# Cross-attention's key mask: from PE matmuls into the keys' last row

## The chip, the cores and the metric

The kernel runs on one core of a Trainium2 chip. The core has a matrix engine (PE, TensorE), a vector engine (DVE), a scalar engine (ACT), a general one (POOL, GpSimd) and a queue that only issues DMAs here (SP). The metric is device time in microseconds. The kernel before took 2411.13 us, the median of three runs (2407.03 to 2411.5).

## The reference, cut to what matters

Four attention blocks follow one another on a batch of 8 sequences of 256 rows and 128 features. The third, L2, holds nearly all of the time: six layers, each with self-attention, cross-attention to 64 context rows of 64 features, and a feed-forward part. The change touches cross-attention alone:

```python
tn = _ln(t, norm_g, norm_b)
t = _mha(src, tn, ckv, cq, cow, cob, src_mask) + t
# _ln(x, g, b):  (x - m) / jnp.sqrt(v + eps) * g + b
# in _mha, 16 heads of 64:
q = t @ q_w
k, v = jnp.split(s @ kv_w, 2, axis=-1)
scores = jnp.einsum('bhqd,bhkd->bhqk', q, k) * D ** (-0.5)
scores = jnp.where(mask[:, None] == 0, jnp.float32(-1000000000.0), scores)
attn = jax.nn.softmax(scores, axis=-1)
```

The mask has one row of 64 keys for each sequence, the same for all heads and queries.

## The kernel before, in words

**Folded weights.** Each layer multiplies the query weights into the key weights (`AT`) and the output weights into the value weights (`WVO`) once, in `plan_ca_weights`. A sequence's keys are then `AT` times its context: a tile of 128 features by 16 heads by 64 keys, made in `keys_both` for two sequences at a time. Scores are the normalised rows, turned so that features lie on the partitions (`tT`), times these keys.

**Ticks and phases.** The program is a list of steps. `at(tick, phase, step)` files a step; at the end all steps are recorded in order of tick, then of phase, and that order is forced on PE, DVE, ACT and POOL each. Every one of these engines so runs strictly in the order of the plan, whatever is ready; only SP's DMAs are placed by the scheduler. Self-attention takes four ticks for a sequence, cross-attention two. Below, T is the first tick of a layer's cross-attention (`T_ca` in the code), so sequence b has the ticks T+2b and T+2b+1, and self-attention of the last sequence starts at T-4.

**One cross-attention tick** (`plan_weights_64`, with a mask): PE makes scores (phase 1); ACT copies them out of PSUM (L372), DVE takes the maximum for each head (L374), POOL subtracts it (L375) (phase 2); ACT takes the exponential (L381, phase 8). In the next tick DVE sums and inverts (L385, L386) and POOL multiplies (L387) (phase 2.4). In the tick after that DVE transposes (L395, phase 2.5), and in the third PE multiplies by the values (`sums`, L429, phase 3). A scores step is 16 matmuls of 128 rows by 32 columns with 256 moving columns in float32 (L356), four at a time on the four column groups of the array, and behind each four of them four more in bfloat16 (L363) that add the mask: a row of ones times a row with 0 or -1e30. Each float32 matmul has two records in the trace.

**Normalisation** (`ahead`): DVE takes the moments, POOL the inverse root (L859, L862), ACT normalises (L868), PE transposes (L882), and ACT takes the transpose out of PSUM with the norm's scale and bias (L884). Self-attention of the next layer does its normalising on DVE (L873), at phase 2.6, behind that tick's transposes.

**One self-attention tick**: DVE adds the mask and takes the maximum in eight instructions (L953), ACT takes exponentials (L958), DVE inverts their sums (L966), POOL divides (L968), DVE transposes (L978), PE multiplies by the values (L994). `out_proj` is L1012, its addition L1019.

**PSUM** is a ring of four buffers of two banks: each new tile takes the buffer of the fourth tile before it, and waits until that one was read. The heap's tags ("q", "o", "k", "e") are rings of four in SBUF in the same way.

**The weights of a layer's cross-attention**, with W = T-6 as the start: DVE transposes them (L1057) at W-6 and W-5; SP sends them through DRAM and back (L1060, L1068); POOL regroups them (L1074) at W+1, phase 8.05; PE makes `AT` at W+2 and `WVO` at W+3, both at phase 3.6 (L1083), and ACT takes them out of PSUM (L1095, L1093). The first `keys_both` (L1120, copied out by L1126) is at T-2, phase 3.7.

Of the kernel before, what the change touches and what calls it, by code (L numbers as in the profile page):

```python
# [8 lines left out]
F32 = mybir.dt.float32  # L9
I32 = mybir.dt.int32  # L10
BF16 = mybir.dt.bfloat16
# [5 lines left out]
P = 128  # L17
# [10 lines left out]
def tile_xattn_stack(ctx: ExitStack, tc: tile.TileContext, io, out: bass.AP):  # L28
# [124 lines left out]

    norm_g = column("L2_norm_g")
    norm_b = column("L2_norm_b")
    pre_g = load_const("L2_pre_gT", [D, NL])
    pre_b = load_const("L2_pre_bT", [D, NL])
    ff_b1 = load_const("L2_ff_b1T", [P, NL, FF // P])
# [103 lines left out]
        return nm  # L262


    nm2 = const.tile([P, B, M], BF16, tag="nm2", name="nm2")
    nc.vector.memset(nm2, 0.0)
    ones0 = const.tile([P, 32], BF16, tag="ones0", name="ones0")
    nc.vector.memset(ones0, 0.0)
    nc.vector.memset(ones0[0:1], 1.0)


    def stats(xin, eps):
# [21 lines left out]
    def at(tick, phase, fn):  # L294
        plan.setdefault(tick, []).append((phase, fn))
# [30 lines left out]
        )  # L326
        return vw

    def plan_weights_64(tick, qt, qT, keys, values, mask, take):

        tl = {}

        def scores():
            sc = two_banks("sc").rearrange("p (q x) -> p q x", q=4)
            if mask is None:
                for i in range(4):
                    for a in range(4):
                        q = (i + 2 * (a // 2)) % 4  # L340
                        rows = slice(64 * (a // 2), 64 * (a // 2) + 64)
                        qb = 4 * qt + q
                        nc.tensor.matmul(
                            sc[32 * a : 32 * a + 32, q, :],
                            lhsT=qT()[rows, qb * 32 : (qb + 1) * 32],
                            rhs=keys()[rows, 4 * (a % 2) : 4 * (a % 2) + 4, :].rearrange(
                                "p h k -> p (h k)"
                            ),
                            start=True, stop=True,
                        )  # L350
                tl["sc"] = sc.rearrange("p q x -> p (q x)")
                return
            for q in range(4):
                qb = 4 * qt + q
                for a in range(4):
                    nc.tensor.matmul(  # L356
                        sc[32 * a : 32 * a + 32, q, :],
                        lhsT=qT()[:, qb * 32 : (qb + 1) * 32],
                        rhs=keys()[:, a].rearrange("p h k -> p (h k)"),
                        start=True, stop=False,  # L360
                    )
                for a in range(4):
                    nc.tensor.matmul(  # L363
                        sc[32 * a : 32 * a + 32, q, :], lhsT=ones0, rhs=mask,
                        start=False, stop=True,
                    )
            tl["sc"] = sc.rearrange("p q x -> p (q x)")

        def lower():
            sc = tl.pop("sc")  # L370
            e = big("e", shape=(P, 16, M))
            nc.scalar.copy(e.rearrange("p h k -> p (h k)"), sc)  # L372
            m = sm([P, 16], "m16")
            nc.vector.tensor_reduce(m, e, AX.X, ALU.max)  # L374
            nc.gpsimd.tensor_tensor(  # L375
                e, e, m.unsqueeze(2).to_broadcast([P, 16, M]), ALU.subtract
            )
            tl["e"] = e

        def exps():  # L380
            nc.scalar.activation(tl["e"], tl["e"], AF.Exp)  # L381

        def divide():
            r = sm([P, 16], "r16")
            nc.vector.tensor_reduce(r, tl["e"], AX.X, ALU.add)  # L385
            nc.vector.reciprocal(r, r)  # L386
            nc.gpsimd.tensor_tensor(  # L387
                tl["e"], tl["e"], r.unsqueeze(2).to_broadcast([P, 16, M]), ALU.mult
            )

        def turn():
            e = tl.pop("e").rearrange("p (q h) (k x) -> p (h k) q x", q=4, x=32)
            eT = big("k" if mask is None else "o", shape=(P, 8, 4, 32))
            for i in range(2):
                nc.vector.transpose(eT[:, 4 * i : 4 * i + 4], e[:, 4 * i : 4 * i + 4])  # L395
            tl["eT"] = eT

        def sums_by_head():

            ps = two_banks("mm").rearrange("p (i x) -> p i x", i=2)  # L400
            eT, vw = tl.pop("eT"), values()
            for i in range(2):
                for k in range(2):
                    for j in range(4):
                        nc.tensor.matmul(
                            ps[32 * j : 32 * j + 32, i, :P],
                            lhsT=cones.rearrange("p a f -> p (a f)") if i == 0
                            else vw[:, 4 * k + j, :],
                            rhs=eT[:, 2 * j + k].rearrange("p q x -> p (q x)"),
                            start=(k == 0), stop=(k == 1),  # L410
                        )
# [24 lines left out]
        at(tick, 2, lower)  # L436
        if mask is None:
            at(tick + 1, 2.05, exps)
            at(tick + 1, 2.5, turn)
            at(tick + 2, 1.9, sums_by_head)  # L440
            at(tick + 2, 4.6, outputs)
        else:
            at(tick, 8, exps)
            at(tick + 1, 2.4, divide)
            at(tick + 2, 2.5, turn)
            at(tick + 3, 3.0, sums)
# [188 lines left out]

    def mask_keys():
        mi = big("q", dtype=I32)
        mi = mi[0:1, : B * M].rearrange("p (b m) -> p b m", b=B)
        nc.sync.dma_start(out=mi, in_=io["mask_Bx1xS2_if1"].rearrange("b o m -> o b m"))
        nc.vector.tensor_scalar(nm2[0:1], mi, 0.0, -BIG, ALU.is_equal, ALU.mult)  # L640

    mask_bf = []

# [39 lines left out]
    def plan_l0(b, T):  # L683
# [87 lines left out]
        at(T + 1, 3.2, make_values)  # L771
        for qt in range(QT):
            plan_weights_64(
                T + qt, qt, lambda: st["q"], lambda: st["k"], lambda: st["VW"], None,
                lambda ps, qt=qt: add(qt, ps),
            )
        at(T + 3, 6, moments)
# [268 lines left out]
    def plan_ca_weights(l, T):  # L1046
# [54 lines left out]
            at(T - 4 + i, -0.5, lambda i=i: fetched(i))  # L1101
        at(T + 1, 8.05, regrouped)
        at(T + 2, 3.6, folded("AT", 0, lambda c: st[1][:, :, c, :], HD ** -0.5))
        at(T + 3, 3.6, folded("WVO", 1, lambda c: W["ca", l][2][:, c, :]))

    keys_of = {}

    def plan_ca(l, b, T):
# [3 lines left out]
        def keys_both():  # L1112
# [16 lines left out]
                    )  # L1129
            keys_of[b], keys_of[b + 1] = res  # L1130

        def make_values():
            st["VW"] = values_of(b, fold["WVO"])

        def res():
            st["tb"] = residual(b, W["ca", l][3])

        ahead(b, (T - 4, 6), (T - 3, 2.95), (T - 2, 2.9), norm_g, norm_b, st)
        if b % 2 == 0:
            at(T - 2, 3.7, keys_both)  # L1140
        at(T + 2, 3.2, make_values)
        at(T + 2, 7, res)

        def add(qt, ps):
            nc.vector.tensor_add(t[:, QT * b + qt, :], ps[:, :D], st["tb"][:, qt, :])  # L1145

        for qt in range(QT):
            plan_weights_64(
                T + qt, qt, lambda: st["tT"], lambda: keys_of[b], lambda: st["VW"],
                nm2[:, b].unsqueeze(1).to_broadcast([P, 4, M]), lambda ps, qt=qt: add(qt, ps),  # L1150
            )

    def plan_ff(l, b, T, T_second, steps=None):
# [117 lines left out]
    for l in range(NL):  # L1271
        T_ca = T0 + 4 * B
        T_next = T_ca + 2 * B
        for b in range(B):
            plan_sa(l, b, T0 + 4 * b)
        plan_ca_weights(l, T_ca - 6)
        for b in range(B):
            plan_ca(l, b, T_ca + 2 * b)
            T_ff = T_ca + 2 * b + 7
# [101 lines left out]
```

## Time and profile before

| what | value |
|---|---|
| median of three runs | 2411.13 us |
| the profiled execution | 2410.29 us, span 2408.5 us, mean PE clock 0.987 |
| ACT busy | 1707.7 us, 71% |
| POOL busy | 1359.1 us, 56% |
| weight loads of PE (PEld) | 1719.9 us, 71% |

The profile is of one execution. Its rows give for a group of equal instructions the busy time and the mean duration of one in ns, and behind the last bar how long the engine had been idle before them and what ended that. Matmuls overlap, so that a mean duration is not what one costs; the distance between starts is.

The second layer is followed as the example. In its timeline the scores of the ticks start at these times, in us:

| tick | T-5 | T-4 | T-3 | T-2 | T-1 | T | T+1 | T+2 | T+3 | T+4 |
|---|---|---|---|---|---|---|---|---|---|---|
| start | 731.33 | 738.72 | 743.33 | 752.00 | 760.31 | 765.84 | 768.50 | 775.41 | 785.28 | 789.56 |

| tick | T+5 | T+6 | T+7 | T+8 | T+9 | T+10 | T+11 | T+12 | T+13 | T+14 | T+15 |
|---|---|---|---|---|---|---|---|---|---|---|---|
| start | 795.06 | 799.35 | 810.68 | 816.70 | 822.47 | 830.27 | 837.95 | 847.54 | 858.62 | 868.15 | 875.38 |

### The profile page before, as it was taken

How to read it: one execution, taken by the hardware profiler on the slowest of the kernel's cores; microseconds unless marked ns; L12 is line 12 of the kernel's file. 1: busy time of each engine (PE TensorE's matmuls, PEld its weight loads, DVE VectorE, ACT ScalarE, POOL GpSimd, SP SyncE). 2: the span in 40 equal slices, each digit the busy share in tenths (PEclk: the TensorE clock that was granted, in tenths of full speed). 3: DMA queues.
4: the chain of work that ended last, by engine and by line, in shares of the span. 5: the costliest groups of instructions: out<-in, count | busy, mean ns of one | idle time of the engine just before them, and what ended most of it. 6: DMA issues, size and time to landing. Idle time of an engine off the chain costs nothing.

```text
span 2408.5 us, 100346 instructions
## 1 busy us (share of the span) xinstructions
PE 2325.2 (97%) x42564; PEld 1719.9 (71%) x42564; DVE 1872.3 (78%) x6237; ACT 1707.7 (71%) x4514; POOL 1359.1 (56%) x2231
## 2 busy tenths in 40 slices
PE   7889999999999999999999999999999999999997
PEld 4557777777777777777777777777777777777775
DVE  5677887777888767888767888767888767888775
ACT  4567777667777667778667778667778667777663
POOL 2444556754556754555764555755555765455665
PEclk9989999999999999999999999999999999999998
DMA  6000022001022001012000012000013000001000
GB/s 180 2 2 20 21 73 65 2 3 30 21 64 66 11 3 30 21 56 73 12 2 26 21 45 87 12 2 18 25 40 89 21 2 18 25 26 42 2 4 16
DMA packets 102834, 76.90 MB, mean 32 GB/s; under 512 B 8113, under 2 KB 96881, under 8 KB 102386
## 3 DMA queue, kind: packets, MB, share of 16 engines
q1 hardware_dynamic: 101794, 70.16, 10.1%
q8 instruction: 335, 5.49, 0.9%
q14 instruction: 113, 0.93, 0.1%
q10 hardware_dynamic: 592, 0.33, 0.1%
HBM read 62.07 MB, written 8.39 MB: 29 GB/s over the span
## 4 chain that ended last, share of the span: by engine, by line
PE 75%; DVE 13%; ACT 5%; POOL 4%; issue 2%; DMA 0%; SPq 0%; POOLq 0%; ACTq 0%; DVEq 0%
PE sc L939 12%; PE mm L902 12%; PE mm L994 12%; PE mm L1012 6%; PE mm L921 6%; PE mm L429 6%; PE sc L356 5%; DVE e L953 3%; PE mm L1178 3%; PE mm L1161 3%; DVE eTc L978 2%; DVE m L374 2%; POOL e L968 2%; PE mm L1120 2%; PE mm L318 2%
## 5 line engine op out<-in xcount | busy, mean ns | idle before, releaser
L968 POOL TENSOR_SCALAR e<-e,rs 128x256 f32<-128x256 f32 x1536 | 702.8, 478 | 706.3 <-DVE rs L966 696.5
L958 ACT ACTIVATE e<-e,mn 128x256 f32<-128x256 f32 x1536 | 758.6, 495 | 151.3 <-DVE mn L953 146.5
L953 DVE CUSTOM_DVE_ANT_0 e<-sc,nm 128x256 f32<-128x256 f32 x1536 | 543.1, 419 | 93.4 <-PE sc L939 92.3
L978 DVE STREAM_TRANSPOSE eTc<-e 128x512 f32<-128x512 f32 x768 | 516.2, 694 | 59.4 <-POOL e L968 58.2
L939 PE MATMUL sc<-k,q 64*32 64x256 f32 x12288 | 380.8, 383 | 2.3 <-DVE o L299 1.3
L994 PE MATMUL mm<-eTc,v 32*64 32x256 f32 x12288 | 363.4, 378 | 5.7 <-ACT AT L1095 3.3
L375 POOL TENSOR_TENSOR e<-e,m 128x1024 f32<-128x1024 f32 x112 | 213.0, 1902 | 262.1 <-DVE m L374 262.1
L994 PEld LDWEIGHTS mm<-eTc,v 32*64 32x64 f32 x12288 | 277.1, 131 | 88.5 <-issue 22.2
L939 PEld LDWEIGHTS sc<-k,q 64*32 64x32 f32 x12288 | 221.8, 107 | 125.3 <-issue 51.4
L374 DVE TENSOR_REDUCE m<-e 128x16 f32<-128x1024 f32 x112 | 136.3, 1217 | 197.0 <-ACT e L372 197.0
L958 ACT ACTIVATION_READ_ACCUMULATOR e<-e,mn 128x1 f32 x1536 | 287.9, 187 | 0.0
L356 PE MATMUL sc<-q,tT 128*32 128x256 f32 x3072 | 217.0, 382 | 3.8 <-DVE t L1019 3.2
L429 PE MATMUL mm<-v,o 128*128 128x128 f32 x1536 | 197.5, 283 | 1.9 <-DVE t L1145 1.7
L429 PEld LDWEIGHTS mm<-v,o 128*128 128x128 f32 x1536 | 183.1, 195 | 19.0 <-issue 9.1
L902 PE MATMUL mm<-tT,w_sk 128*128 128x256 f32 x768 | 189.2, 389 | 0.2 <-PE mm L994 0.2
L1012 PEld LDWEIGHTS mm<-w_sow,o 128*128 128x128 f32 x1536 | 175.1, 192 | 17.6 <-issue 12.3
L921 PE MATMUL mm<-w_sv,tT 128*32 128x256 f32 x3072 | 185.6, 382 | 0.0
L1012 PE MATMUL mm<-w_sow,o 128*128 128x128 f32 x1536 | 183.6, 278 | 1.3 <-ACT WVO L1093 1.3
L387 POOL TENSOR_TENSOR e<-e,r 128x1024 f32<-128x1024 f32 x96 | 182.6, 1902 | 0.5 <-DVE r L386 0.5
L301 ACT COPY v<-mm 128x1024 f32<-128x1024 f32 x96 | 97.1, 1012 | 115.4 <-PE mm L921 115.4
L902 PE MATMUL mm<-tT,w_sq 128*128 128x256 f32 x768 | 173.6, 379 | 0.0
L902 PEld LDWEIGHTS mm<-tT,w_sk 128*128 128x128 f32 x768 | 138.3, 190 | 44.2 <-issue 29.2
(222 smaller groups left out, 3489.4 us busy)
## 6 DMA issues: line engine op xcount, KB each, us to landing
nm<-mask_d SPq DMA_DIRECT2D x192, 128.0 KB
wd<-o SPq DMA_DIRECT2D x48, 128.0 KB
w_sk<-in_L_sa_kv_dram SPq DMA_DIRECT2D x6, 512.0 KB
w_sv<-in_L_sa_kv_dram SPq DMA_DIRECT2D x24, 128.0 KB
w_sq<-in_L_sa_q_dram SPq DMA_DIRECT2D x6, 512.0 KB
w_sow<-in_L_sa_ow_dram SPq DMA_DIRECT2D x6, 512.0 KB
w_ckv<-in_L_ca_kv_dram SPq DMA_DIRECT2D x12, 256.0 KB
w_cq<-in_L_ca_q_dram SPq DMA_DIRECT2D x6, 512.0 KB
```

What stands on the lines that cost most here:

```text
L356: nc.tensor.matmul(sc[32 * a : 32 * a + 32, q, :], lhsT=qT()[:, qb * 32 : (qb + 1) * 32], rhs=keys()[:, a].rearrange("p h k -> p (h k)"), ...
L375: nc.gpsimd.tensor_tensor(e, e, m.unsqueeze(2).to_broadcast([P, 16, M]), ALU.subtract)
L429: nc.tensor.matmul(ps[:, :D], lhsT=eT[:, s].rearrange("p q x -> p (q x)"), rhs=vw[:, r, k, g, :], start=(s == 0), stop=(s == 7),)
L902: nc.tensor.matmul(ps[:, i * S : (i + 1) * S], lhsT=w[:, c * P : (c + 1) * P], rhs=st["tT"], start=True, stop=True,)
L921: nc.tensor.matmul(ps[32 * a : 32 * a + 32, i, :], lhsT=st["tT"][:, kb * 32 : (kb + 1) * 32], rhs=sv[:, a].rearrange("p g x -> p (g x)"), ...
L939: nc.tensor.matmul(sc[32 * a : 32 * a + 32, r, j, :], lhsT=st["q"][g][rows, a, qb * 32 : (qb + 1) * 32], rhs=st["k"][g][rows, a, :], start ...
L953: nc.vector.tensor_tensor_reduce(e[:, i, :], sc4[:, i, :], st["nm"][:, 2 * jj + i % 2, :], -1.0, 3.0 * BIG, ALU.add, ALU.min, mn[:, i : i ...
L958: nc.scalar.activation(e[:, i, :], e[:, i, :], AF.Exp, scale=-1.0, bias=mn[:, i : i + 1], accum_out=rs[:, i : i + 1],)
L968: nc.gpsimd.tensor_scalar(e[:, i, :], e[:, i, :], rs[:, i : i + 1], 1.0, ALU.mult, ALU.mult)
L978: nc.vector.transpose(eT[:, r, :, 2 * jj : 2 * jj + 2, :], e[:, 2 * r : 2 * r + 2, :].rearrange("p j (k x) -> p k j x", x=32),)
L994: nc.tensor.matmul(ops[a // 2][r * HD : (r + 1) * HD, a % 2, :S], lhsT=st["v"][kb // 4][rows, kb % 4, (2 * g + r) * HD : (2 * g + r + 1) * ...
L1012: nc.tensor.matmul(st["ps"][:, j * D : (j + 1) * D], lhsT=st["oT"][c // 4][:, c % 4, j * P : (j + 1) * P], rhs=sow[:, c, :], start=(c == 0 ...
```

## The change

A normalised row sums to zero over its features. So its last feature says nothing that the others don't, and its place can carry a constant 1: every other feature's key weight then has the last one's subtracted. The change does this: `tT` keeps features 0 to 126 without the norm's scale and bias and has 1 in row 127; the norm's scale is multiplied into `AT`, the last column is subtracted from all, and what the norm's bias adds to a score becomes the last column. The mask is then added to the last row of a sequence's keys, in SBUF, by one DVE instruction over 32 partitions (96 to 127) and 1024 columns, of which 31 partitions get a zero. The 16 mask matmuls of each scores step are gone.

The start of the weights' plan moves from T-6 to T-7, so their transposes, their way through DRAM, the regrouping and `AT` are one tick earlier; `WVO` stays at T-3. Between `AT` at T-5 and the first keys at T-2 come five new steps: a product for the bias (`meet_bias`, T-5), the scaling (`scale`, T-4), the subtraction of the last column (`lose_last`, T-4), the sum for the bias (`sum_bias`, T-4, on DVE) and its place (`put_bias`, T-3); all but the sum are POOL's. Two rows of norm constants are loaded to all partitions at the start, and the mask is loaded to 128 partitions and not to one.

```diff
-                        start=True, stop=False,
-                    )
-                for a in range(4):
-                    nc.tensor.matmul(
-                        sc[32 * a : 32 * a + 32, q, :], lhsT=ones0, rhs=mask,
-                        start=False, stop=True,
+                        start=True, stop=True,
                     )
...
-        at(T + 3, 3.6, folded("WVO", 1, lambda c: W["ca", l][2][:, c, :]))
+
+        def rows(i):
+            return norm_rows[:, i].unsqueeze(1).to_broadcast([P, HC, D])
+
+        def meet_bias():
+            st["z"] = big("q", shape=(P, HC, D))
+            nc.gpsimd.tensor_tensor(st["z"], st["AT"], rows(1), ALU.mult)
+
+        def sum_bias():
+            st["add"] = sm([P, HC], "add")
+            nc.vector.tensor_reduce(st["add"], st.pop("z"), AX.X, ALU.add)
+
+        def scale():
+            nc.gpsimd.tensor_tensor(st["AT"], st["AT"], rows(0), ALU.mult)
+
+        def lose_last():
+            last = sm([P, HC], "last")
+            nc.gpsimd.tensor_copy(last, st["AT"][:, :, D - 1])
+            nc.gpsimd.tensor_tensor(
+                st["AT"], st["AT"], last.unsqueeze(2).to_broadcast([P, HC, D]), ALU.subtract
+            )
+
+        def put_bias():
+            nc.gpsimd.tensor_copy(st["AT"][:, :, D - 1], st.pop("add"))
+
+        at(T + 2, 8.05, meet_bias)
+        at(T + 3, 2.35, scale)
+        at(T + 3, 8.05, lose_last)
+        at(T + 3, 8.7, sum_bias)
+        at(T + 4, -0.1, put_bias)
+        at(T + 4, 3.6, folded("WVO", 1, lambda c: W["ca", l][2][:, c, :]))
...
+        def mask_keys():
+            last = keys_of[b][96:].rearrange("p a c k -> p (a c) k")
+            nc.vector.tensor_tensor(
+                last, last, nm2[96:, b].unsqueeze(1).to_broadcast([32, 16, M]), ALU.add
+            )
+
...
-        ahead(b, (T - 4, 6), (T - 3, 2.95), (T - 2, 2.9), norm_g, norm_b, st)
+        ahead(b, (T - 4, 6), (T - 3, 2.95), (T - 2, 2.9), last_off, last_on, st)
         if b % 2 == 0:
             at(T - 2, 3.7, keys_both)
+        at(T - 1, 1.9, mask_keys)
...
-        plan_ca_weights(l, T_ca - 6)
+        plan_ca_weights(l, T_ca - 7)
```

In this diff T is each plan's own start: in `plan_ca` it is T+2b of the text, so that the mask of sequence b is added at T+2b-1, phase 1.9, ahead of that tick's maximum (phase 2).

More of the change, by code (lines that the diff above doesn't have):

```diff
@@ L155, in tile_xattn_stack @@
     norm_b = column("L2_norm_b")
+    norm_rows = const.tile([P, 2, D], F32, tag="norm_rows", name="norm_rows")
+    for i, name in enumerate(("L2_norm_g", "L2_norm_b")):
+        nc.sync.dma_start(out=norm_rows[:, i, :], in_=io[name].partition_broadcast(P))
     pre_g = load_const("L2_pre_gT", [D, NL])
@@ L262, in load_mask @@
         return nm
[L265 to L269, printed above, removed]
+    nm2 = const.tile([P, B, M], F32, tag="nm2", name="nm2")
+    last_on = ident[:, P - 1 : P]
+    last_off = const.tile([P, 1], F32, tag="last_off", name="last_off")
+    nc.vector.tensor_scalar(last_off, last_on, -1.0, 1.0, ALU.mult, ALU.add)
+    last_big = const.tile([P, 1], F32, tag="last_big", name="last_big")
+    nc.vector.tensor_scalar(last_big, last_on, -BIG, None, ALU.mult)
     def stats(xin, eps):
@@ L327, in values_of, with plan_weights_64 @@
         return vw
-    def plan_weights_64(tick, qt, qT, keys, values, mask, take):
+    def plan_weights_64(tick, qt, qT, keys, values, halves, take):
         tl = {}
@@ L336, in scores @@
             sc = two_banks("sc").rearrange("p (q x) -> p q x", q=4)
-            if mask is None:
+            if halves:
                 for i in range(4):
@@ L392, in turn @@
             e = tl.pop("e").rearrange("p (q h) (k x) -> p (h k) q x", q=4, x=32)
-            eT = big("k" if mask is None else "o", shape=(P, 8, 4, 32))
+            eT = big("k" if halves else "o", shape=(P, 8, 4, 32))
             for i in range(2):
@@ L436, in plan_weights_64 @@
         at(tick, 2, lower)
-        if mask is None:
+        if halves:
             at(tick + 1, 2.05, exps)
@@ L637, in mask_keys @@
         mi = big("q", dtype=I32)
-        mi = mi[0:1, : B * M].rearrange("p (b m) -> p b m", b=B)
-        nc.sync.dma_start(out=mi, in_=io["mask_Bx1xS2_if1"].rearrange("b o m -> o b m"))
-        nc.vector.tensor_scalar(nm2[0:1], mi, 0.0, -BIG, ALU.is_equal, ALU.mult)
+        mi = mi[:, : B * M].rearrange("p (b m) -> p b m", b=B)
+        nc.sync.dma_start(
+            out=mi, in_=io["mask_Bx1xS2_if1"].rearrange("b o m -> (b o) m").partition_broadcast(P)
+        )
+        nc.vector.tensor_scalar(nm2, mi, 0.0, last_big, ALU.is_equal, ALU.mult)
     mask_bf = []
@@ L773, in plan_l0 @@
             plan_weights_64(
-                T + qt, qt, lambda: st["q"], lambda: st["k"], lambda: st["VW"], None,
+                T + qt, qt, lambda: st["q"], lambda: st["k"], lambda: st["VW"], True,
                 lambda ps, qt=qt: add(qt, ps),
@@ L1130, in keys_both @@
             keys_of[b], keys_of[b + 1] = res
+        def mask_keys():
+            last = keys_of[b][96:].rearrange("p a c k -> p (a c) k")
+            nc.vector.tensor_tensor(
+                last, last, nm2[96:, b].unsqueeze(1).to_broadcast([32, 16, M]), ALU.add
+            )
         def make_values():
@@ L1149, in plan_ca @@
                 T + qt, qt, lambda: st["tT"], lambda: keys_of[b], lambda: st["VW"],
-                nm2[:, b].unsqueeze(1).to_broadcast([P, 4, M]), lambda ps, qt=qt: add(qt, ps),
+                False, lambda ps, qt=qt: add(qt, ps),
             )
```

## The prediction, made before the run

> **What bounds the kernel now.** The busy line and the chain of waits come first.
>
> ```profile
> PE 2325.2 (97%) x42564; PEld 1719.9 (71%) x42564; DVE 1872.3 (78%) x6237; ACT 1707.7 (71%) x4514; POOL 1359.1 (56%) x2231
> ...
> PE 75%; DVE 13%; ACT 5%; POOL 4%; issue 2%; DMA 0%; SPq 0%; POOLq 0%; ACTq 0%; DVEq 0%
> ```
>
> PE is the bound on average, but a quarter of the chain is elsewhere. The question is whether that quarter lies where the change adds work. The timeline of the second layer answers it (the layers repeat: PE waits for DVE L1019 in six places, once in each). First PE's own price:
>
> ```profile
> 775.41 0.64 PE L356 MATMUL sc<-q,tT 128*32 128x256 f32 x8
> 775.87 0.29 PE L363 MATMUL sc<-nm,ones 128*32 128x256 bf16 x4
> 775.98 0.61 PE L356 MATMUL sc<-q,tT 128*32 128x256 f32 x8
> ...
> 777.72 0.44 PE L882 MATMUL tp<-ident,xn 128*128 128x128 f32 x2
> ...
> 706.58 1.93 PE L921 MATMUL mm<-w_sv,tT 128*32 128x256 f32 x32
> 708.44 0.44 PE L882 MATMUL tp<-ident,xn 128*128 128x128 f32 x2
> ```
>
> From start to start a scores step takes 2.31 us with its mask matmuls. L921 is the same 16 matmuls without any: 1.86. (L363's busy sum, 112.4 us, overlaps its neighbours; four mask matmuls delay the next by 0.11.)
>
> Now the places where PE isn't the bound:
>
> ```profile
> 739.92 0.42 DVE L953 CUSTOM_DVE_ANT_0 e<-sc,nm 128x256 f32<-128x256 f32 x1 [0.59 <-PE sc L939]
> ...
> 761.51 0.43 DVE L953 CUSTOM_DVE_ANT_0 e<-sc,nm 128x256 f32<-128x256 f32 x1 [1.09 <-PE sc L939]
> ...
> 821.01 1.22 DVE L374 TENSOR_REDUCE m<-e 128x16 f32<-128x1024 f32 x1 [2.90 <-ACT e L372]
> ...
> 827.15 1.21 DVE L374 TENSOR_REDUCE m<-e 128x16 f32<-128x1024 f32 x1
> ...
> 846.69 0.30 PE L882 MATMUL tp<-ident,xn 128*128 128x128 f32 x1 [0.88 <-DVE xn L873]
> ```
>
> From T-4 (739.92) to T-1 (760.42) DVE is idle 0.8 us in all, waiting for POOL: it is full. From T to T+4 maxima follow each other at 5.23 us (769.29, 774.52, 779.74): maximum 1.14, POOL's subtraction 1.9, exponential 0.96, the next copy 1.0, and handovers. From T+8 (821.01) to T+9 and on to 831.4 DVE is full again, and at T+12 PE waits 1.17 us (0.88 and 0.29) for L873, which ends DVE's tick T+11.
>
> **Part by part, the second layer.** Shifts are against the times before.
>
> *Removed:* 16 steps x (2.31 - 1.86, taken as 0.44) = 7.0 us a layer, 42.2 in all, at most 0.55 a step where the following weight load hides too. It reaches the end only where PE isn't waiting.
>
> *The fold one tick earlier.* AT's 32 matmuls (741.44 to 743.33, 1.89 us) now stand in front of T-4's scores, for which DVE already waits 0.59. DVE starts T-4 at 741.8: **+1.9**. Since DVE is full from there to 760.42, it does not get this back: what counts there is DVE's work, not PE's. PE's waits for the regrouping (0.76), AT's and WVO's evictions (0.54, 0.23) go, but PE then waits for DVE. T-4 now holds only scores for PE, so that it is through `values` at 749.6; WVO's two PSUM buffers are those of T-3's scores, and their maxima start at 746.65 + 1.9 + 1.15 (next edit) = 749.7 and last 2.75 us, to 752.4. PE stands still for 2.8 us; cover gone, this is what DVE's lateness costs it. The transposes L1057 move between like ticks, zero. Their DMAs pass SP one tick earlier: fetches were issued at 695.90 and 705.02, the mask load `nm` behind them at 706.53; earlier is no harm, 0 to -0.9.
>
> *sum_bias,* one reduction as L374 (1217 ns, 1.15 to the next start), stands ahead of T-3's maxima in full DVE: **+1.15**.
>
> *POOL:* three 128x1024 products as L375 (1902 ns) and two small copies (as L862, 0.2). `meet_bias` fits behind T-5's divides. `scale` delays T-4's second divide to 749.7-751.5, needed at 752.4: hidden. Then 751.5 + 2.1 (`lose_last`) + 0.9 (L859, L862) + 0.2 (`put_bias`) hold POOL to 754.8; T-3's divide was due at 753.7, and DVE's transpose, which waits for its first half, is with it **+1.0** late (0 if POOL is quicker, 2.1 if `lose_last` counts in full). ACT's normalising of the first rows waits for the same L862, 0.5 late, with room behind it.
>
> *mask_keys of b=0* at T-1: 1.15 us, from 32 partitions but 1024 columns (nearest row L631, 1207 ns for one such addition, an operand in PSUM). It waits for keys that ACT copied at 759.53 to 761.5 before and that now come with PE's late T-2, **+0.5** beyond DVE's own lateness (0 if it only waits for the third of four copies), and stands ahead of eight maxima. Before, 1.09 us were idle there. T-1's maxima: 1.9 + 1.15 + 1.0 + 0.5 + 1.15 - 1.09 = +4.6. T's maximum had 0.98 idle in front; ACT's queue leaves 0.8 of it: **+3.8**. The 5.23 us loop has no slack, so it carries that through T+2 to L1019, whose PSUM buffer PE's scores of T+3 need (0.55 waited there already).
>
> *Other masks.* b=1 (1.74 idle ahead) and b=2 (3.51) hide in the wait for ACT's copy, but for 0.2 at the port; a hidden one costs its 1.15 where that wait is gone. T+3's scores: -0.44. b=3 at T+5: DVE comes straight from two sets of moments, no idle, +1.25 with the port. So `sums` at T+6 (804.12, where PE waited 0.27 for DVE): 3.8 + 0.2 - 0.44 + 1.25 = **+4.8**. Then T+7's scores -0.44, b=4 hides (2.47), b=5 at T+9 +1.15 (no idle), b=6 at T+11 +0.7 (0.44 idle), port +0.2: **+1.6** at L873, so at PE's T+12. The rows 821.01 to 827.15 show why PE's own gain doesn't help here: DVE alone needs 6.14 us from one maximum to the next. T+12 to T+15 and the self-attention behind them are PE's (windows without any idle PE time): 4 x -0.44 = **-1.76**; b=7 hides in 5.92 idle.
>
> A layer: 4.8 + 1.6 - 1.76 = +4.6; five of them 23.2. In the last there is no L873: +4.8 to T+6, then zero (between -4.4, ten PE-bound steps, and +1.6). Start: two loads of 64 KB and a mask of 256 instead of 2 KB, issued at 119.2 and needed at 140.7: 0 to +1. Sum +28 on 2410.29, the profiled execution's time, which is 0.84 under the median: **2438 us**.
>
> *A rule against the change.* The row first:
>
> ```profile
> L873 DVE TENSOR_SCALAR xn<-t,mv,rstd x96: 305/505/1431, 103.3 to 2182.3; 128x128 f32<-128x128 f32 x96
> ```
>
> Equal work takes 305 to 1431 ns; at 845.12 two took 2.11 us while POOL's L387 ran. The Trainium skill ("SBUF — State Buffer", Who interferes with whom) says that a DVE instruction with two SBUF inputs shares a read port with POOL, and whoever comes second waits for the whole instruction. `mask_keys` has two SBUF inputs; no row here shows one of its size. By L631 alone a mask costs 1.15 flat: the sum falls by 0.5 a layer, to 2435. By the rule masks b=3, 5, 6, which meet POOL's L859 (698 ns), wait up to 0.7 each: 2.1 instead of 0.5 a layer, 2447. I take the small share since L859 is often through.
>
> **Rivals.**
> *PE stays the bound (faster).* Masks fall into DVE's idle time before a maximum (197.0 us over 112, 1.76 each, more than 1.15), and the fold's earlier start only removes PE waits: -42.2 - 6 x 1.53 = 2359. For it: 97% and "ACT e" ahead of most maxima. Against: T+5 and T+9 have none, and PE waits for DVE at T+12 already. It decides if DVE is through before PE's T+12 transposes. Partial forms reach 2405. Chance 0.20.
>
> *Only the masks cost.* If DVE catches up after T-4: b=0 +0.6 at T's maximum, 0.2 - 0.44 + 1.25, +1.6, -1.76: +1.4 a layer, 2419 (2405 to 2426). For it: DVE's 0.8 us of POOL waits shows that not all there is work. Against: the empty tick T-4. Chance 0.18.
>
> *The clock, too.*
>
> ```profile
> 800.00:804.00 4.00, 2.60 (x44) 1.33 (x36) 3.97 (x8) 2.20 (x5) 3.84 (x6) 1.00 0.00 0
> 804.00:808.00 4.00, 3.88 (x32) 3.45 (x40) 2.59 (x5) 2.33 (x4) 2.54 (x2) 0.57 0.01 4
> ```
>
> After 1.4 us without PE work the granted clock (third number from the end) falls to 0.57 and `sums` takes 3.43 us instead of 1.95: 1.5 lost. My walk leaves PE idle some 2.8 us before WVO; one such fall more a layer is +9: 2447. Chance 0.14, the forecast (2425 to 2442) 0.48.
>
> **Numbers.** About 0.2% can be told from no change. Slower: 0.48 + 0.14 + most of 0.18 = 0.73; same 0.05; faster 0.22. The range leaves out most of the first rival below and the port's worst with the clock above: 2400 to 2458; the forecast's own is 2425 to 2442.
>
> **What would show it.** L363 gone and PE's busy sum some 40 us lower; DVE's first L953 of T-4 idle over 2 us; PE waiting for DVE (or its PSUM) before WVO; PE's wait for L873 at T+12 grown from 1.2 us to over 3. Wrong if that wait has not grown, or if T-4's late start is made up by T-1.

## The result, and the profile after

| what | before | after |
|---|---|---|
| median | 2410.32 us (6 runs) | 2429.49 us (6 runs, 2428.49 to 2432.91) |
| the profiled execution, and its span | 2410.29, 2408.5 us | 2432.91, 2431.1 us |
| mean PE clock of that execution | 0.987 | 0.982 |

The ratio is 1.0086 (95% interval 1.0075 to 1.0096): the change makes the kernel slower by 19 us, or 22.6 between the two spans. The page's busy line and its chain of waits by engine, after:

```profile
PE 2301.6 (95%) x41028; PEld 1688.9 (69%) x41028; DVE 1941.5 (80%) x6290; ACT 1706.2 (70%) x4514; POOL 1439.6 (59%) x2261
...
PE 71%; DVE 14%; POOL 6%; ACT 6%; issue 2%; DMA 0%; POOLq 0%; ACTq 0%; DVEq 0%
```

The 1536 mask matmuls are gone, DVE and POOL are busy 69 and 80 us longer, and PE's share of the chain falls from 75 to 71%, while POOL's grows from 4 to 6. The list of PE's waits (instruction, releaser, sum, times, longest, in us) says for what PE now stands:

```profile
PE tp L885 <- DVE xn L876: 16.2, 10, 2.9
PE mm L1086 <- DVE mn L956: 13.9, 11, 1.6
PE mm L997 <- DVE eTc L981: 13.6, 12, 1.1
PE sc L362 <- DVE q L1167: 13.6, 6, 2.3
```

All four end on DVE. Before, the first (there L882 for L873) was 5.9 us. In code lines, L956 is before's L953 (self-attention's maxima), L981 is L978, L876 is L873, L1086 is L1083, and L1167 is the new mask addition.

**From T-4 to T.** PE's timeline of the second layer, whose T-5 starts 6.67 us later than before:

```profile
745.39 1.96 PE L1086 MATMUL mm<-w_cq,o 64*64 64x128 f32 x32
747.28 3.69 PE L942 MATMUL sc<-k,q 64*32 64x256 f32 x128
752.10 4.21 PE L997 MATMUL mm<-eTc,v 32*64 32x256 f32 x128 [1.13 <-DVE eTc L981]
757.91 0.40 PE L1086 MATMUL mm<-w_cow,o 64*64 64x128 f32 x2 [1.61 <-DVE mn L956]
759.29 3.64 PE L1086 MATMUL mm<-w_cow,o 64*64 64x128 f32 x30 [0.98 <-DVE mn L956]
762.86 3.10 PE L942 MATMUL sc<-k,q 64*32 64x256 f32 x64
```

`AT` stands in front of T-4's scores (which share a row with T-3's), and PE then runs out of work: it waits 1.61 and 0.98 us ahead of `WVO` for DVE's maxima to free PSUM. Behind the pause it is slow here: 30 matmuls of `WVO` take 3.64 us and T-2's scores 3.10 (before 1.97 for all 32 and 1.96). The granted clock of this stage (741 to 776) is 0.90, that of the same stage before 1.00. Not all layers do this: in the last four the same two waits stand there (1.6 and 1.0 us), and the 30 matmuls take 1.93 us. DVE's timeline:

```profile
748.48 0.43 DVE L956 CUSTOM_DVE_ANT_0 e<-sc,nm 128x256 f32<-128x256 f32 x1 [2.48 <-PE sc L942]
...
755.21 1.18 DVE L1117 TENSOR_REDUCE add<-q 128x8 f32<-128x1024 f32 x1
756.31 0.41 DVE L956 CUSTOM_DVE_ANT_0 e<-sc,nm 128x256 f32<-128x256 f32 x1
...
762.79 0.71 DVE L981 STREAM_TRANSPOSE eTc<-e 128x512 f32<-128x512 f32 x1 [1.72 <-POOL e L971]
...
772.64 1.22 DVE L1167 TENSOR_TENSOR q<-q,nm 32x1024 f32<-32x1024 f32 x1 [0.61 <-ACT q L1159]
773.89 0.42 DVE L956 CUSTOM_DVE_ANT_0 e<-sc,nm 128x256 f32<-128x256 f32 x1
```

DVE now waits 2.48 us for T-4's first scores (0.59 before); ahead of T-3's maxima stands `sum_bias`; T-3's transposes wait 1.72 us for POOL; and ahead of T-1's maxima stands the first mask. POOL's timeline says why it was late:

```profile
754.50 2.35 POOL L1120 TENSOR_TENSOR AT<-AT,norm_rows 128x1024 f32<-128x1024 f32 x1
756.84 1.84 POOL L971 TENSOR_SCALAR e<-e,rs 128x256 f32<-128x256 f32 x4
758.62 0.19 POOL L1124 COPY last<-AT 128x8 f32<-128x8 f32 x1
758.90 1.90 POOL L1125 TENSOR_TENSOR AT<-AT,last 128x1024 f32<-128x1024 f32 x1
760.75 0.70 POOL L862 TENSOR_TENSOR rstd<-ve,mhalf 128x2 f32<-128x2 f32 x1
761.53 0.20 POOL L865 TENSOR_TENSOR nm<-mneg,rstd 128x2 f32<-128x2 f32 x1
761.66 0.20 POOL L1130 COPY AT<-add 128x8 f32<-128x8 f32 x1
761.83 1.84 POOL L971 TENSOR_SCALAR e<-e,rs 128x256 f32<-128x256 f32 x4
```

T-3's divides (761.83) stand behind `lose_last`, the norm and `put_bias`; these lines follow each other with hardly a gap.

**From T+5 to T+6.** PE's timeline after, then before's:

```profile
812.53 3.19 PE L362 MATMUL sc<-q,tT 128*32 128x256 f32 x32 [2.26 <-DVE q L1167]
815.66 1.03 PE L885 MATMUL tp<-ident,xn 128*128 128x128 f32 x4
816.52 1.97 PE L430 MATMUL mm<-v,o 128*128 128x128 f32 x16
```

```profile
802.91 0.94 PE L882 MATMUL tp<-ident,xn 128*128 128x128 f32 x4 [1.20 <-ACT xn L868]
804.12 3.43 PE L429 MATMUL mm<-v,o 128*128 128x128 f32 x16 [0.27 <-DVE t L1145]
```

The scores of T+6 wait 2.26 us for the mask of b=3, which DVE makes from 811.17 to 812.39, and then run slow. Before, PE's pause came behind the scores, and `sums` ran slow. The wait is the same in all six layers; the scores are slow behind it in five (all but the first), and before's `sums` in four (all but the third and the fifth).

**T+12.** PE's timeline:

```profile
858.82 0.30 PE L885 MATMUL tp<-ident,xn 128*128 128x128 f32 x1 [2.94 <-DVE xn L876]
859.41 0.33 PE L885 MATMUL tp<-ident,xn 128*128 128x128 f32 x1 [0.29 <-DVE xn L876]
```

The wait of 1.17 us has grown to 3.23.

**The start.** 2.5 of the 22.6 us are there before the first layer's second sequence (209.26 to 211.76). No row shows a new wait there; the same scores behind the same wait run at another clock, first before, then after:

```profile
24.63 1.93 PE L343 MATMUL sc<-q,xn 64*32 64x256 f32 x32 [2.16 <-DVE o L549]
```

```profile
25.41 3.64 PE L349 MATMUL sc<-q,xn 64*32 64x256 f32 x32 [2.16 <-DVE o L550]
```

The profiled executions of before, after and the ten versions below reach this place between 205.5 and 211.8 us (e7, which is after up to here, at 205.67), so I count it to the execution and not to the change. It is most of the distance between the profiled execution and after's median (3.4 us).

### The profile page after: what moved, and what is told of

It reads as the page before. It is cut to its first block, busy times and chain, and to the rows that moved or that the text cites. A ratio compares the mean times of both kernels' runs of the same rounds, so it can differ in the third digit from the quotient of the medians.

```text
span 2431.1 us, 97351 instructions
## 1 busy us (share of the span) xinstructions
PE 2301.6 (95%) x41028; PEld 1688.9 (69%) x41028; DVE 1941.5 (80%) x6290; ACT 1706.2 (70%) x4514; POOL 1439.6 (59%) x2261
## 4 chain that ended last, share of the span: by engine, by line
PE 71%; DVE 14%; POOL 6%; ACT 6%; issue 2%; DMA 0%; POOLq 0%; ACTq 0%; DVEq 0%
PE mm L905 14%; PE sc L942 13%; PE mm L997 12%; PE mm L924 7%; PE mm L1015 7%; PE mm L430 4%; DVE m L375 3%; PE sc L362 3%; PE mm L1218 3%; PE mm L1201 3%; POOL e L376 2%; ACT e L373 2%; DVE e L956 2%; DVE o L396 1%; DVE r L386 1%
## 5 line engine op out<-in xcount | busy, mean ns | idle before, releaser
L956 DVE CUSTOM_DVE_ANT_0 e<-sc,nm 128x256 f32<-128x256 f32 x1536 | 543.5, 419 | 96.5 <-PE sc L942 94.5
L981 DVE STREAM_TRANSPOSE eTc<-e 128x512 f32<-128x512 f32 x768 | 516.3, 695 | 70.7 <-POOL e L971 69.6
L997 PE MATMUL mm<-eTc,v 32*64 32x256 f32 x12288 | 362.1, 377 | 13.6 <-DVE eTc L981 13.6
L376 POOL TENSOR_TENSOR e<-e,m 128x1024 f32<-128x1024 f32 x112 | 213.0, 1902 | 225.0 <-DVE m L375 225.0
L997 PEld LDWEIGHTS mm<-eTc,v 32*64 32x64 f32 x12288 | 277.0, 131 | 95.7 <-issue 33.9
L375 DVE TENSOR_REDUCE m<-e 128x16 f32<-128x1024 f32 x112 | 136.5, 1218 | 134.6 <-ACT e L373 133.8
L362 PE MATMUL sc<-q,tT 128*32 128x256 f32 x3072 | 192.7, 393 | 18.9 <-DVE q L1167 13.6
L1015 PEld LDWEIGHTS mm<-w_sow,o 128*128 128x128 f32 x1536 | 175.1, 192 | 19.7 <-issue 12.3
L388 POOL TENSOR_TENSOR e<-e,r 128x1024 f32<-128x1024 f32 x96 | 182.6, 1902 | 0.5 <-DVE r L387 0.5
```

The costliest lines, as they stand in the source:

```text
L362: nc.tensor.matmul(sc[32 * a : 32 * a + 32, q, :], lhsT=qT()[:, qb * 32 : (qb + 1) * 32], rhs=keys()[:, a].rearrange("p h k -> p (h k)"), ...
L376: nc.gpsimd.tensor_tensor(e, e, m.unsqueeze(2).to_broadcast([P, 16, M]), ALU.subtract)
L956: nc.vector.tensor_tensor_reduce(e[:, i, :], sc4[:, i, :], st["nm"][:, 2 * jj + i % 2, :], -1.0, 3.0 * BIG, ALU.add, ALU.min, mn[:, i : i ...
L981: nc.vector.transpose(eT[:, r, :, 2 * jj : 2 * jj + 2, :], e[:, 2 * r : 2 * r + 2, :].rearrange("p j (k x) -> p k j x", x=32),)
L997: nc.tensor.matmul(ops[a // 2][r * HD : (r + 1) * HD, a % 2, :S], lhsT=st["v"][kb // 4][rows, kb % 4, (2 * g + r) * HD : (2 * g + r + 1) * ...
L1015: nc.tensor.matmul(st["ps"][:, j * D : (j + 1) * D], lhsT=st["oT"][c // 4][:, c % 4, j * P : (j + 1) * P], rhs=sow[:, c, :], start=(c == 0 ...
```

## The experiments

**Theory A**, the prediction's: what the removed matmuls give back is only what PE does where nothing holds it (T+3, T+7, T+12 to T+15), and DVE's and POOL's new work costs where DVE has no idle time. **Rivals**: PE is the bound, so that removal alone brings its whole 42 us; the masks alone cost it all; or the shared read port does. Each kernel was measured in five rounds beside before, whose median in the three groups of runs was 2409.3 (e1 to e4), 2409.6 (e5 to e8) and 2408.9 (e9, e10). Within a version the slower executions show the lower granted clock: those of e1 reach from 2408.1 us at 0.986 to 2417.4 at 0.980. So 3 us between two versions are no sign of a cause by themselves.

| version | us | ratio to before, 95% interval |
|---|---|---|
| e3: before, no mask matmuls | 2391.38 | 0.9929 (0.9915 to 0.9942) |
| e1: after, old tick of the fold, no five steps | 2414.08 | 1.0020 (1.0013 to 1.0026) |
| e4: after, no five steps | 2421.48 | 1.0054 (1.0040 to 1.0067) |
| after | 2429.49 | 1.0086 (1.0075 to 1.0096) |
| e2: after, no mask on DVE | 2409.79 | 1.0004 (0.9996 to 1.0012) |
| e7: after, mask step with one input | 2427.84 | 1.0080 (1.0068 to 1.0093) |
| e6: steps on the weights, old tick of the fold | 2410.39 | 1.0007 (0.9999 to 1.0016) |
| e5: e6, masks by PE | 2407.56 | 0.9995 (0.9986 to 1.0003) |
| e8: e6, masks of odd b a tick earlier | 2420.02 | 1.0044 (1.0031 to 1.0057) |
| e9: e6, mask of b=5 a tick earlier | 2405.32 | 0.9988 (0.9981 to 0.9994) |
| e10: e6, masks of b=2 to 5 by PE | 2406.91 | 0.9992 (0.9984 to 1.0000) |

**e3, the removal alone.**

```diff
-                        start=True, stop=False,
-                    )
-                for a in range(4):
-                    nc.tensor.matmul(
-                        sc[32 * a : 32 * a + 32, q, :], lhsT=ones0, rhs=mask,
-                        start=False, stop=True,
+                        start=True, stop=True,
```

> The kernel before without its mask matmuls: the mask is left out. What the removal alone is worth. Theory A (PE is held by DVE at T+1, T+3, T+6 and T+12, so only part of 0.44 us a step comes through: T, T+3, about two of the steps T+7 to T+11, and T+12 to T+15, some 3.5 us a layer): 2389 us (2380 to 2398). Rival (PE bounds everywhere): 42 us less, 2368.

2391.38, so 18 of PE's 42 us: the rival with PE as the bound falls. The waits of PE in this version:

```profile
PE tp L877 <- ACT xn L863: 13.4, 13, 2.1
PE tp L877 <- DVE xn L868: 6.4, 10, 1.0
```

The first was 9.7 before, the second 5.9: part of what PE saves is waited away for rows that it then needs sooner.

**e1, removal and masks on DVE.**

```diff
-        at(T + 2, 8.05, meet_bias)
-        at(T + 3, 2.35, scale)
-        at(T + 3, 8.05, lose_last)
-        at(T + 3, 8.7, sum_bias)
-        at(T + 4, -0.1, put_bias)
-        at(T + 4, 3.6, folded("WVO", 1, lambda c: W["ca", l][2][:, c, :]))
+        at(T + 3, 3.6, folded("WVO", 1, lambda c: W["ca", l][2][:, c, :]))
...
-        plan_ca_weights(l, T_ca - 7)
+        plan_ca_weights(l, T_ca - 6)
```

> The changed kernel with the key weights folded where they were before (regrouped at T-5, AT at T-4, WVO at T-3) and without the five new steps; the keys' mask stays on DVE. It leaves out the norm's scale and bias and the subtraction of the last column. Theory A (the fold's earlier tick and its steps make DVE late from T-4 to T, 4.7 us a layer, and the masks eat PE's gain behind it): the lateness at T falls from 4.7 to about 0.4 us a layer, so some 22 us less, 2407 us (2400 to 2414). Rival B (the masks on DVE are the whole loss, the fold is hidden): 2425 to 2431, as the changed kernel.

2414.08 is just over the upper edge. Against e3 it carries the 48 masks on DVE (and the longer loads at the start): 22.7 us, 3.8 a layer. PE's waits for the mask (13.6 us, 6 times) and for L876 (15.5) are there already.

**e2, the mask on DVE left out of after.**

```diff
-        at(T - 1, 1.9, mask_keys)
```

> The changed kernel without mask_keys: the mask is left out. Theory A: 0.8 us a layer less at T, the waits of T+6 (2.3) and T+12 (2.9) fall back, but the fold's lateness of about 3.9 us stays: 2411 us (2405 to 2418). Rival B: all of the loss goes and PE's 42 us come in part, 2385 or less. Rival C (the adds lie in idle time and cost nothing): 2425 to 2431.

2409.79, as expected. Seen from this side the masks cost 19.7 us.

**e4, the early tick without the five steps.**

```diff
-        at(T + 2, 8.05, meet_bias)
-        at(T + 3, 2.35, scale)
-        at(T + 3, 8.05, lose_last)
-        at(T + 3, 8.7, sum_bias)
-        at(T + 4, -0.1, put_bias)
```

> The changed kernel with the fold one tick early (AT at T-5, WVO at T-3) but without the five new steps; it leaves out the norm's scale and bias and the subtraction of the last column. Theory A: the empty tick T-4 alone keeps DVE 1.9 us late, of which DVE's idle 1.1 us at T-1 is already used by the first mask: 1.5 to 1.9 us a layer over the run with the old fold, 2417 us (2412 to 2421). Rival (the steps on POOL and DVE are the whole loss): 2407, as the old fold. Rival (the early tick is the whole loss): 2425 to 2431.

2421.48, just over the upper edge again. Against e1 the early tick alone costs 7.4 us, and against after the five steps cost 8.0. The row of parts is so -18, +22.7, +7.4, +8.0, together +20; after's median is 19 to 20 above before's. The rival by which only the masks cost falls: without early tick and steps the change would stand at 2414.

**e7, one SBUF input.** The step copies the keys' last row onto itself by a reduction over one element, on DVE, of the same shape and in the same place.

```diff
-            nc.vector.tensor_tensor(
-                last, last, nm2[96:, b].unsqueeze(1).to_broadcast([32, 16, M]), ALU.add
-            )
+            nc.vector.tensor_reduce(last, last.unsqueeze(3), AX.X, ALU.max)
```

> The changed kernel with mask_keys as a copy of the same 32x1024 elements onto themselves by a reduction over one element: the same place, waits and elements on DVE, but one input from SBUF; the mask is left out. If the shared read port costs what the trace of after shows (POOL's L862 and L865 held for 1 us at five of eight masks, most of it off the chain): 2424 to 2429 us, and L862 and L865 back at 0.7 and 0.2 us each time. If the port is much of the loss: 2420 or less. If it costs nothing: as the changed kernel, 2429 to 2431, with L862 still held.

2427.84, 1.7 us less, with intervals of the ratio that overlap (1.0075 to 1.0096 and 1.0068 to 1.0093): at the end the port costs little or nothing. The groups of both versions, first after, then e7:

```profile
L862 POOL TENSOR_TENSOR rstd<-ve,mhalf 128x2 f32<-128x2 f32 x144 | 116.9, 812 | 15.6 <-DVE ve L855 10.1 <-DVE mneg L858 5.0
...
L865 POOL TENSOR_TENSOR nm<-mneg,rstd 128x2 f32<-128x2 f32 x96 | 41.3, 430 | 7.5
```

```profile
L862 POOL TENSOR_TENSOR rstd<-ve,mhalf 128x2 f32<-128x2 f32 x144 | 100.4, 697 | 15.6 <-DVE ve L855 10.1 <-DVE mneg L858 5.0
...
L865 POOL TENSOR_TENSOR nm<-mneg,rstd 128x2 f32<-128x2 f32 x96 | 18.7, 195 | 7.5
```

With one input POOL's two small steps have before's means of 698 and 195 ns to 1 ns. With two inputs they take 39 us more: the collision is there, but in after the mask mostly comes first (its 48 additions take 1.22 us in the median, 1.64 at most), and it is POOL that is held. That it has time there is what the small difference says.

**e6, the five steps elsewhere.** They work on the turned query weights before `AT` is made, at T-9 to T-7, where DVE has more room; `AT` is at T-4 again, and `z` has a buffer of its own.

```diff
-        at(T + 2, 3.6, folded("AT", 0, lambda c: st[1][:, :, c, :], HD ** -0.5))
+        at(T + 3, 3.6, folded("AT", 0, lambda c: st[1][:, :, c, :], HD ** -0.5))
...
+        at(T - 2, 8.05, meet_bias)
+        at(T - 1, 8.05, scale)
+        at(T - 1, 8.7, sum_bias)
+        at(T, 8.05, lose_last)
```

> The five steps work on the turned query weights between T-9 and T-7, AT is back at T-4, the keys' mask stays on DVE. Theory A (sum_bias and POOL's steps cost only where DVE is full, T-4 to T-1): as the run with the old fold and no steps, 2414 us, up to 3 more. Rival (their work costs wherever it stands): 2421 or over.

2410.39, under the expectation: the steps cost nothing where DVE isn't full, and the version is if anything a little faster than e1, which hasn't got them. Their intervals overlap, and it goes with the clock: e1's eight executions at 0.984 or more took 2408.1 to 2412.0 us, e6's twelve 2409.0 to 2411.8; e1 has thirteen below 0.984, e6 one. The work of `z`, the scaling and the subtraction is the same here (2.37, 2.37 and 1.91 us on POOL): after's 15 us of early tick and steps were their place, not their length.

**e5, the masks by PE.** On top of e6, PE puts the mask into the keys' last row as it makes them, by two bfloat16 matmuls for each half of a pair's keys.

```diff
+                for r in range(2):
+                    nc.tensor.matmul(
+                        ps[:, r], lhsT=into_last,
+                        rhs=nm2[:, b : b + 2].rearrange("p b m -> p (b m)")
+                        .unsqueeze(1).to_broadcast([P, 4, 2 * M]),
+                        start=True, stop=False,
+                    )
...
-                            start=True, stop=True,
+                            start=False, stop=(a == 3),
...
-        at(T - 1, 1.9, mask_keys)
```

> The five steps work on the turned query weights between T-9 and T-7, AT is back at T-4, and the mask goes into the keys' last row while PE makes them: 4 matmuls of 512 columns in bfloat16 for two sequences (0.85 us), none on DVE. Theory A: the kernel before without mask matmuls took 2391; four times 0.85 us in six layers are 20 if all of it counts, and the one at T+2 should lie partly in a wait of PE: 2404 us (2397 to 2412), below the kernel before. Rival (the steps still make DVE late, wherever they stand): 8 us more, 2412 or over.

2407.56. The 0.85 us in the expectation are an estimate: L363's four at once, of 256 columns, delay the next by 0.11 us, so one of 512 columns would take 0.22 and four 0.88; they take 1.06 (e10 has the rows). PE pays nearly as much for these matmuls as DVE did for the additions, and the interval holds 1. PE's wait for L876 is back at 6.2 us.

**e8, masks of odd b one tick earlier.** By theory A the masks of b=3 and b=5 should leave their full ticks.

```diff
-        at(T - 1, 1.9, mask_keys)
+        at(T - 1 - b % 2, 1.9, mask_keys)
```

> As the run with the steps on the weights, but the odd sequences' masks are added one tick earlier, T+2b-2 and not T+2b-1, where DVE waited 1.3 to 3.3 us ahead of the maximum before. Theory A (a mask costs where DVE comes to it without a wait: T+5, T+9, T+11): the waits of PE's scores for mask b=3 at T+6 (2.3 us a layer) go, b=5 hides, b=6 at T+11 stays: 1.2 to 2.4 us a layer less, 7 to 14 us below the run with the steps on the weights, 2403 to 2409. Rival (a mask costs its DVE time anywhere): no change against that run.

2420.02: a miss by 11 us and more. DVE's timeline of it:

```profile
770.51 1.22 DVE L1170 TENSOR_TENSOR q<-q,nm 32x1024 f32<-32x1024 f32 x1
771.77 1.22 DVE L375 TENSOR_REDUCE m<-e 128x16 f32<-128x1024 f32 x1
...
795.33 2.15 DVE L1170 TENSOR_TENSOR q<-q,nm 32x1024 f32<-32x1024 f32 x1
...
821.38 2.15 DVE L1170 TENSOR_TENSOR q<-q,nm 32x1024 f32<-32x1024 f32 x1
```

The mask of b=1 now stands right ahead of T's maximum, where nothing is idle, and moves the whole 5.23 us loop: L997 at T+1 waits 2.48 us for DVE, 1.11 in e6. And at T+4 and T+8 the mask begins while POOL's L388 runs and takes 2.15 us, not 1.22. The expectation had left out b=1, and that DVE pays when POOL is first. Four masks were moved at once; e9 moves one.

**e9, the mask of b=5 alone.**

```diff
-        at(T - 1, 1.9, mask_keys)
+        at(T - 1 - (b == 5), 1.9, mask_keys)
```

> Like the version with the five steps on the turned query weights (2410.4 us), but the mask of the sixth sequence alone (b=5) is added one tick earlier, at T+8, where DVE has some 2 us without work; the other seven stay. Theory A (a mask costs its duration where DVE's work decides and nothing where DVE waits, and is 0.9 us longer where it meets POOL's product at the port): DVE loses 1.2 us at T+9, PE's wait for the normalised rows at T+12 falls by about 1 us a layer: 2403 to 2407. Rival (the order of the pool's and DVE's other work absorbs it, or the collision at T+8 gives it back): 2409 to 2412. A time above 2414 would mean that the step at T+8 is itself on the path.

2405.32, within theory A's range and out of the rival's. DVE's timeline from T+8 to T+9, first e6, whose mask is at T+9:

```profile
824.83 1.22 DVE L1170 TENSOR_TENSOR q<-q,nm 32x1024 f32<-32x1024 f32 x1
826.08 1.22 DVE L375 TENSOR_REDUCE m<-e 128x16 f32<-128x1024 f32 x1
```

```profile
816.84 2.15 DVE L1170 TENSOR_TENSOR q<-q,nm 32x1024 f32<-32x1024 f32 x1
819.24 1.22 DVE L375 TENSOR_REDUCE m<-e 128x16 f32<-128x1024 f32 x1 [0.25 <-ACT e L373]
...
825.38 1.21 DVE L375 TENSOR_REDUCE m<-e 128x16 f32<-128x1024 f32 x1
```

The 2.15 us mask fits into T+8's wait and leaves 0.25 of it; T+9's maximum is 0.70 us earlier than in e6 although this layer began 0.67 later (T+6's maxima: 812.84 and 812.17), so 1.37 gained. PE's waits for L876 fall from 15.6 to 12.7 us. Of the versions that keep the mask this is the only one whose interval lies wholly under 1, by about 0.1% of before: it beats both kernels, but hardly.

**e10, four masks by PE.** The two masks without idle time in front (b=3, b=5) and their pairs' others are put in by PE as in e5, those of b=0, 1, 6, 7 by DVE.

```diff
+                by_pe = b in (2, 4)
...
+        if b // 2 in (0, 3):
+            at(T - 1, 1.9, mask_keys)
```

> The same base, with the masks of b=2 to 5 put in by PE with the keys (two bfloat16 matmuls of 512 columns for each half of a pair's keys) and those of b=0, 1, 6, 7 by DVE. Theory A: the two masks that met DVE without idle time (b=3 at T+5, b=5 at T+9) are gone from DVE, so PE waits for no mask at T+6; left are 0.1 to 0.6 us for b=0 and 0.7 for b=6 a layer, and PE's own 4 matmuls for two pairs, about 0.9 us each, partly in its waits: 2399 to 2406, below the 2407.6 of the version with all masks by PE. Rival (what PE pays for the masks is cheap and what DVE pays for b=0 and b=6 dear): 2408 to 2411.

2406.91, just out of theory A's range, and out of the rival's. PE's timeline shows the price of two matmuls, 0.53 us to the next start, 1.06 for a pair:

```profile
780.58 0.61 PE L1162 MATMUL mm<-nm,into_last 128*128 128x512 bf16 x2
781.11 1.16 PE L1171 MATMUL mm<-ctx,AT 64*128 64x128 f32 x16
```

PE's wait for the mask at T+6 is gone, as expected, but the gain on e6 is 3.5 us, not 4 to 11.

## Why the prediction was right, and where its terms were off

The direction and the mechanism held: forecast +28, measured +22.6 on the spans and +19 on the medians. Of its four signs three came (DVE idle for 2.48 us at T-4, PE waiting ahead of `WVO`, 3.23 us at T+12); PE's busy sum did not fall by 40. The terms for the second layer, each from after's times less the 6.67 us that it began later, and the same for the other five:

| term | predicted | second layer | other layers |
|---|---|---|---|
| DVE's start of T-4 | +1.9 | +1.89 (748.48 for 739.92) | +1.9 |
| with `sum_bias`, T-3's maxima | +3.05 | +2.99 (756.31 for 746.65) | +3.0 |
| with POOL's queue, T-2's maxima | +4.05 | +4.90 (764.92 for 753.35) | +4.3 |
| with the mask of b=0, T-1's maxima | +4.6 | +5.7 (773.89 for 761.51) | +5.1 |
| T's maximum | +3.8 | +4.7 (780.65 for 769.29) | +4.1 |
| T+3's scores | +4.0 | +4.68 (796.63 for 785.28) | +4.1 |
| start of `sums` of T+6 | +4.8 | +5.73 (816.52 for 804.12) | +5.1 |
| the matmuls behind `sums` | +4.8 | +4.27 (818.42 for 807.48) | +3.9 to +4.2; +5.1 and +5.2 in the third and fifth |
| from there to T+12's transposes | +1.6 | +1.2 (859.41 for 847.28) | +0.7 to +1.0 |
| T+12 to the next layer's scores | -1.76 | -1.75 (895.76 for 885.38) | -1.75; -0.1 in the first |
| a layer | +4.6 | +3.7 | +4.7, +4.3, +3.1, +4.4 |

The last layer has no T+12 of this kind, so the last three rows have four layers beside the second.

- **What removal brings.** -0.44 at T+3 and T+7 and -1.76 at T+12 to T+15 are 2.6 a layer, 15.8 in six, close to the 18 of e3. In the first layer T+12's scores run slow (3.54 us for 1.93), and its gain is lost.
- **The idle PE ahead of `WVO`** was there: 2.6 us (1.61 and 0.98) for the 2.8 predicted, in every layer.
- **The first mask's wait** for ACT's keys was put at 0.5 us and is 0.61.
- **POOL's queue was sized too small.** `scale` began where the prediction has it (754.50, which is 747.83 in before's times), but `scale` and `meet_bias` were taken at L375's 1.90 us and take 2.36 and 2.38. T-3's divides start 1.33 us later than DVE's lateness explains (761.83, against 750.84 + 6.67 + 2.99), for 1.0 predicted. This makes +4.3 at T-2's maxima, and five layers have just that. In the second DVE waits for PE on top of it:

```profile
764.92 0.42 DVE L956 CUSTOM_DVE_ANT_0 e<-sc,nm 128x256 f32<-128x256 f32 x1 [0.51 <-PE sc L942]
```

- **The clock at `WVO`** was priced as a rival, +9 for one such fall a layer. It fell in two layers: the 30 matmuls took 2.96 us in the first, 3.64 in the second, and 1.93 in the last four (granted clock in the 4 us from the start of these matmuls: 0.50 in the second layer, 1.00 in the third). The third layer's rows:

```profile
1131.87 1.93 PE L1086 MATMUL mm<-w_cow,o 64*64 64x128 f32 x30 [0.98 <-DVE mn L956]
1133.73 1.09 PE L942 MATMUL sc<-k,q 64*32 64x256 f32 x32
1135.88 1.10 PE L942 MATMUL sc<-k,q 64*32 64x256 f32 x32 [1.06 <-ACT o L307]
```

  Where they are quick, PE waits 1.06 us for ACT amid T-2's scores instead. From `AT` to T-2's keys it is 23.6 us in all layers but the second, which takes 24.45. The fall so cost 0.6 us at T-2's maxima of one layer, which stay in its later rows, and not 1.5 in each.
- **The fall at T+6 was given back by the clock.** The prediction let the whole shift pass through T+6, and it named `sums` as what waits; it is the scores of T+6, in front of it, that wait for b=3's mask, 2.26 us. Whether they then run slow changes nothing: in the first layer they take 1.93 us, and `sums` waits 0.80 us for DVE and starts at the same +5.1 as in the layers with 2.92 to 3.10. But behind this earlier pause `sums` itself is near full clock in all layers (1.97 to 2.18 us). Before, it was slow in four (2.95 to 3.43) and at full clock in the third and fifth (2.05). In these two nothing is given back (+5.1 and +5.2 behind it), in the four 0.9 to 1.5 us are. So the gain is before's slow `sums`, not DVE's lateness worked off.
- **PE's busy sum** was to fall by 40 us and fell by 23.6. Before the first layer's T-5 it grew by 3.9, at another clock; from T-5 to T-5 it fell by 3.7 to 5.8 a layer, for the 7.0 removed. In the second layer 3.3 are missing, and its slow stretches are nearly all of that: `WVO` 4.04 in two parts for 1.97 (+2.1), T-2's scores (+1.1), T+6's scores (+1.3), `sums` (-1.5), together +3.0. A busy time isn't work alone; at a lower clock it grows.
- **The sum.** The first T-5 comes 2.2 us late (predicted for the start: 0 to +1), the five layers add 4.4, 3.4, 4.1, 2.7 and 4.1 from T-5 to T-5 (0.3 to 0.4 less than in the table, which ends earlier; predicted 4.6 each), and the last adds 1.7 (predicted 4.8): 22.6. In the last layer the shift is 3.6 at the keys of T+6, so PE's last ticks give 1.9 back, where the prediction had zero, between -4.4 and +1.6. The misses have both signs: the lateness at T+6 was put 0.3 too low for five layers, its growth to T+12 too high by 0.4 to 0.9, and the clock's turns were in no term of the sum. That the sum comes this near is in part luck.
- **Splitting by parts.** Early tick and five steps together were 1.9 + 1.15 + 1.0 = 4.05 a layer in the walk, and 15.4 / 6 = 2.6 in e4 and after; their shifts at T-2 are real, but not all of it arrives behind T+6. What takes it up there besides the clock isn't settled.
- **The rule on the shared port** (the Trainium skill, "SBUF — State Buffer", Who interferes with whom) holds here: the same mask takes 1.22 us alone and 2.15 behind POOL's product (e8, e9), and POOL's small steps wait for it. The sum by the rule was +2.1 a layer on DVE, the sum taken +0.5; e7 measures 1.7 / 6 = 0.3 at the end, which isn't clear of zero. In after the mask is mostly first, so it is POOL that pays.

Of the rivals, PE as the bound is refuted by e3, the masks as the only cost by e4 and e6. The rival with the clock had the fall at `WVO` right in two layers of six, and its price wrong.

## What to carry to other kernels

Before taking work from the busiest engine, count only the stretches where nothing holds it (here 18 of 42 us), and put the price of the replacement at the exact ticks of the other engine: the same DVE addition was free behind a wait of 2 us, cost its 1.2 us in a full tick, and moved a whole loop when it stood ahead of its first maximum. Preparation that a layer needs once belongs where the in-order engines have room, whatever it is counted for (19 us went away by moving the five steps three to four ticks and the fold back by one). And PE can run slower behind a pause, so that a moved pause can give back some of what it took: about 1 us here, in four layers of six. Look at every layer before taking one as the example: in the second the clock cost 0.6 us that the other five don't have.

## What was not expected of the hardware

- POOL's 128x1024 products differ with their second operand: 1.90 us where one value is repeated along the inner axis (L1125, L376), 2.36 to 2.38 where a whole row is repeated for every head (L1113, L1120). The groups of after:

```profile
L1113 POOL TENSOR_TENSOR q<-AT,norm_rows 128x1024 f32<-128x1024 f32 x6 | 14.3, 2376 | 14.7 <-ACT AT L1098 14.7
L1120 POOL TENSOR_TENSOR AT<-AT,norm_rows 128x1024 f32<-128x1024 f32 x6 | 14.2, 2363 | 0.0
...
L1125 POOL TENSOR_TENSOR AT<-AT,last 128x1024 f32<-128x1024 f32 x6 | 11.4, 1896 | 0.5
```

- Whoever comes second at the port pays: POOL's 128x2 steps went to 1.69 us (from 0.70) and to 1.15 (from 0.20) beside a mask that had begun before them, the mask to 2.15 (from 1.22) beside a product of POOL that had.
- The same pause of PE is followed by slow matmuls in one layer and not in another. In after, behind 1.6 and 1.0 us, `WVO`'s 30 take 2.96 and 3.64 us in two layers and 1.93 in four; behind 2.26, T+6's scores take 2.92 to 3.19 in five and 1.93 in one; behind 2.94, T+12's take 3.54 in one and 1.93 in four. The length of the pause alone doesn't decide; what does, no run here shows.
